# Five of eight images combined, a later lead, and fewer weight steps beside combined images, in a 3x3 convolution with quantised weights and group normalisation

## The chip, the cores and the metric

The kernel runs on one core of one Trainium2 chip. The metric is the device time of one execution in microseconds (us). The engines are named as the profile names them: PE multiplies matrices, DVE is the vector engine, ACT the scalar engine, POOL is GpSimd, and SP issues transfers.

## The reference

The input x holds 160 images of 128 channels and 32x32 points. Every image is group-normalised (32 groups of 4 channels, over the points too), convolved 3x3 with padding 1, and added to x:

```python
beta, alpha = jnp.max(U), jnp.min(U)
s1 = (beta - alpha) / 3.0
v1 = s1 * floor(U / s1)
s2 = s1 / 5.0
v2 = s2 * floor((U - v1) / s2)
w = (v1 + v2).reshape(128 * 5, 128, 3, 3)
xb = x.reshape(160 // 5, 5 * 128, 32, 32)
act = conv(xb, w, padding=1, feature_group_count=5)
x = x + act.reshape(160, 128, 32, 32)      # conv takes gn(x)
```

There are five sets of weights. The kernel orders the images by set, 32 to a set, so the weights of the next set have to be quantised, turned and summed while the current set is convolved.

## The kernel before, in words

One image is one step of the loop in `run`. Each image is split into a high part (fp16) and a low remainder (fp16), so that products of fp16 matrices keep enough precision. A Winograd-like scheme along one axis turns three taps on two neighbouring rows (or columns) into four products: two of sums and differences, called `m1` and `m2`, and two that go straight to the even and odd outputs. There are two kinds of image.

- An **uncombined image (U)**: only the low part goes through the scheme. GpSimd (`beside_pairs`, L714) or ScalarE (`normalise`, L640) makes the normalised image z; ScalarE casts it to the high part (L648); VectorE subtracts (L751) and makes the three combinations of rows (L764, L772, L773). PE needs 30 matmuls.
- A **combined image (C)**: both parts go through the scheme. GpSimd makes the outer columns and one quarter of the combination v (L678, L708), VectorE the rest (`combine`, L690 and L697); ScalarE scales it to the high part (L738) and VectorE makes the low part in one instruction (`low_combined`, L744). PE needs 24 matmuls.

`combined(i)` chooses: odd images from 7 to 29, then three of five up to image 129 (`THIRDS`), then three of four.

In its step for image i, PE runs the sums of image i+1 (`sums_of_pairs`, into m2 and m1) and then the two halves of image i itself (`main`). ScalarE copies m2 out (`leave`, L891), and VectorE forms the start values of the next image's two banks from m1 and m2 (`pairs`, L903 and L905: the pair update). PE cannot start the halves of an image before its pair update, nor its sums before its low part.

The other work runs ahead by fixed distances. `step_of(i, ahead)` gives the images whose stage is due in step i: stage 4 is GpSimd's work and `combine`, stage 3 the high part, stage 2 the low part. Up to image `FURTHER` the stages run 4, 3 and 2 images ahead; at a certain step each handles two images, and from then on they run 5, 4 and 3 ahead. This extra image is called the lead. Statistics are measured by ScalarE `STAT_LEAD + 1` images ahead (L241, L248).

Quantising the next weights is a list of short VectorE instructions, the weight steps (L142 to L146, L162, L549; sums of taps L573 to L575), 42 per set. `Later` hands them out at a pace; `take(n)` issues up to n that are due. Before the change a step offers three places beside a U image (two around its low part, one after `combine`) and two beside a C image. At the 28th image of a set `later.finish()` issues what is left.

GpSimd's instructions of stage 4 and the power that gives 1/sqrt of the variance (L286) wait for a VectorE instruction named `before`: the last but one of those issued for the low part. All engines run in the written order.

Images are grouped for the statistics, from 24 on by eight. When a group's power is done, VectorE scales it (L307). If the group's first image is U, ScalarE normalises that image (`by_scalar_too`), and VectorE makes a shift for it (L310).

Of the kernel before, what the change touches and what calls it, by code (L numbers as in the profile page):

```python
# [385 lines left out]
class Main:  # L386
# [21 lines left out]

    STAT_LEAD = 15
    FURTHER = 11
    LOAD_LEAD = 18
    CHUNKS = 11
    STEADY = 7
# [193 lines left out]
    def stats_of(self, k):  # L609
        if k not in self.stats:  # L610
            self.stats[k] = Statistics(
                self.nc, self.small, self.gavg, self.mhalf, len(self.groups[k]),
                self.steps.lift, k,
            )
            self.stats[k].late = self.groups[k].start not in self.HURRIED
            self.stats[k].shifted = not self.combined(self.groups[k].start)
        return self.stats[k]

    def measure(self, i, stages=(0, 1)):
# [31 lines left out]
    def combined(self, i):  # L651

        if i < self.STEADY or i >= self.imgs:
            return False

        if i < self.FIFTHS:
            return i % 2 == 1
        return i % 5 % 2 == 0 if i < self.THIRDS else i % 4 != 2

    def by_scalar_too(self, i):  # L660

        return i < self.FIRST + 4 or i == self.groups[self.group_of[i]].start

    def column_of(self, i):

# [307 lines left out]
    def step_of(self, i, ahead):  # L973


        change = self.FURTHER + 4 - ahead
        return [k for k in range(i + ahead + (i > change), i + ahead + 1 + (i >= change)) if k < self.imgs]

    def consumed(self, c):

        return max(i + 2 if self.by_hand(i) else i - 2 - (i > self.FURTHER + 6) for i in range(c * NB, c * NB + NB))

    def run(self):
# [130 lines left out]
        later, turned = Later(), []  # L1114
        for i in range(self.imgs):
            n, b = self.place(i)


            def on_the_way(col):
                if col == self.COLS[1]:  # L1120
                    for st in ready:
                        st.means(self.pg)
                    for *column, parts in self.columns:
                        self.turn_column(*column, parts)
                        turned.append(column)
                    self.columns.clear()
                if col == self.COLS[2]:
                    for st in middle:
                        st.variances()

            if i < self.FIRST:
                if i == self.FIRST - 1:
                    self.sums_of_pairs(self.FIRST)

                j = (i - 1) % self.FIRST
                self.direct_hi(j, self.COLS[2])
                self.direct_lo(j, self.COLS[2])
                if i == 0:
                    self.stats[2].variances()
                    self.stats[2].deviation()  # L1140
                    self.stats[2].power()
                    self.stats[2].scales()
                    run(self.sums_across(0, nc.gpsimd))
                for col in self.COLS:
                    on_the_way(col)
            else:
                j = i - 1
                self.conv(i, on_the_way)
            ahead = i + min(10 + i // 3, self.STAT_LEAD + 1)
            to_measure = range(measured, min(self.imgs, ahead))  # L1150
            measured += len(to_measure)
            if i == 2:
                self.load_set(1)
            if b == self.per_set - 8 and n + 2 < N_SETS:
                self.load_set(n + 2)
            if n + 1 < N_SETS:
                if b == (4 if n == 0 else 1):
                    later = Later(
                        (s for col in self.COLS for s in self.make_column(n + 1, col, "later")),
                        36 / (self.per_set - 6 - b),  # L1160
                    )
            later.next_image()
            by_scalar = [k for k in to_measure if not self.by_vector(k)]
            by_vector = [k for k in to_measure if self.by_vector(k)]

            if i < self.FIRST:

                if i == 0:
                    measure(0, 8, 9, 10)
                if i == 1:  # L1170
                    self.normalise(4)
                    self.high_part(4)
                if i == 2:
                    self.leave(3)
                    self.normalise(5)
                    measure(1, 9)
                    self.high_part(5)
                    self.pairs(3)
                    self.low_part(4)
                    run(self.combinations(4))  # L1180
                    measure(0, 11)
                self.residual(j)
            else:

                last = None
                for k in self.step_of(i, 2):
                    if self.combined(k):
                        last = last_of(self.low_combined(k), last)
                    else:
                        self.low_part(k)  # L1190
                        later.take(1)
                        last = last_of(self.combinations(k), last)
                last = later.take(1, last)
                if last:
                    before = self.last_but_one(last)
                    for st in scaled:
                        self.after(st.power(), before)
                    for k in self.step_of(i, 4):
                        self.beside_pairs(k, before)
                if i > self.FIRST and self.by_hand(j):  # L1200
                    self.residual(j)
                for k in by_scalar:
                    self.measure(k, (0,))
                if i > self.FIRST and not self.by_hand(j):
                    self.residual(j)
                    self.accumulate(j)
                if i + 1 < self.imgs:
                    self.leave(i + 1)
                for st in ready:
                    if not st.late:  # L1210
                        st.deviations()
                for k in self.step_of(i, 3):
                    if self.combined(k):
                        self.high_combined(k)
                        continue
                    if self.by_scalar_too(k):
                        self.normalise(k)
                    self.high_part(k)
                for k in by_scalar:
                    self.measure(k, (1,))  # L1220
            for st in middle:
                st.deviation()
                if not st.late:
                    st.power()
                    st.scales()
            if i < self.FIRST:
                for st in ready:
                    st.deviations()
            for n_of, col in turned:
                self.keep_taps(n_of, col)  # L1230
                if col == self.COLS[-1]:
                    later = Later(self.sums_of_set(n_of), 3.0)
            turned = []

            if i >= self.FIRST:

                if i + 1 < self.imgs:
                    self.pairs(i + 1)
                for st in scaled:
                    st.scales_by_vector()  # L1240
                for k in self.step_of(i, 4):
                    if self.combined(k):
                        self.combine(k)
                    later.take(1)
                later.take_scalar()
                if b in (self.per_set - 4, self.per_set - 2):
                    later.finish()
                for st in ready:
                    if st.late:
                        st.deviations_by_vector()  # L1250
            scaled, middle, ready = [st for st in middle if st.late], ready, []
            if i >= self.FIRST:
                measure(0, *by_vector)
            for k in to_measure:
                group = self.group_of[k]
                if k + 1 == self.groups[group].stop:
                    ready.append(self.stats[group])
            while loaded * NB < self.imgs and (
                loaded * NB < i + self.LOAD_LEAD if loaded < self.CHUNKS
                else i >= self.consumed(loaded - self.CHUNKS)  # L1260
            ):
                self.load(loaded)
                due.append((i + 4, loaded))
                loaded += 1
            if due and due[0][0] <= i:
                self.store_input(due.pop(0)[1])
# [49 lines left out]
```

## Time and profile before

| | |
|---|---|
| median of three runs | 966.23 us (966.21 to 966.47) |
| the profiled execution | 964.56 us |
| its span | 962.5 us |
| PE busy | 927.8 us, 96% |
| DVE busy | 902.6 us, 94% |
| ACT busy | 862.7 us, 90% |
| POOL busy | 460.1 us, 48% |

The span lies between the first and the last instruction; the rest of the execution is around it. Matmuls are pipelined, so the busy share of PE counts overlapping ones as one stretch; the spacing of their starts tells their pace.

### The profile page before, as it was taken

What the parts mean: (1) busy time and instruction counts of PE and PEld (TensorE: products, weight loads), DVE (VectorE), ACT (ScalarE), POOL (GpSimd) and SP (SyncE); (2) the same over time, 40 slices, a digit from 0 to 9 for tenths busy, and PEclk for the clock granted to TensorE, in tenths of its full rate; (3) what the DMA queues carried; (4) which work ended last, traced back from release to release, by engine and by line L of the source; (5) the groups of instructions that cost most, each with busy time, mean ns of one, the idle gap of its engine ahead of it and who ended that gap; (6) DMA issues with size and microseconds to landing.
All of it is one profiled execution on the core that took longest, in us unless ns stands there. A gap on an engine that the chain in (4) does not pass through costs nothing.

```text
span 962.5 us, 13034 instructions
## 1 busy us (share of the span) xinstructions
PE 927.8 (96%) x4432; PEld 433.8 (45%) x4432; DVE 902.6 (94%) x1269; ACT 862.7 (90%) x1167; POOL 460.1 (48%) x477
## 2 busy tenths in 40 slices
PE   2899989999999999999999999999999999999997
PEld 1344434444444444444444444444444444444443
DVE  7989999999899999989999999899999998999993
ACT  5879989999899999999999999999999999997660
POOL 4344434456445445554545445545444366565640
PEclk9999999999999999999999999999999999999999
DMA  9079999999999999999999999999999999856563
GB/s 349 36 267 345 334 348 320 325 321 325 328 321 323 317 295 308 272 306 254 295 251 289 284 293 297 282 277 286 267 273 267 282 279 269 172 91 107 91 107 112
DMA packets 67450, 254.22 MB, mean 264 GB/s; under 512 B 5296, under 2 KB 5296, under 8 KB 67376
## 3 DMA queue, kind: packets, MB, share of 16 engines
q1 hardware_dynamic: 45344, 173.09, 48.0%
q0 software_dynamic: 22032, 80.23, 44.4%
q8 instruction: 36, 0.59, 0.2%
q14 instruction: 38, 0.31, 0.1%
HBM read 89.19 MB, written 164.10 MB: 263 GB/s over the span
## 4 chain that ended last, share of the span: by engine, by line


## 5 line engine op out<-in xcount | busy, mean ns | idle before, releaser
L788 PE MATMUL eo<-hi,wt 128*128 128x496 f16 (+3 forms) x1170 | 310.8, 376 | 2.4 <-DVE eo L905 1.7
L843 PEld LDWEIGHTS <-wt 128*128 128x128 f16 x1884 | 183.9, 99 | 211.5 <-DVE eo L905 2.7
L744 DVE SCALAR_TENSOR_TENSOR vl<-v,rstd,vh 128x2048 f16<-128x2048 f32 x94 | 221.8, 2360 | 0.2 <-ACT vh L738 0.2
L843 PE MATMUL eo<-vh,wt 128*128 128x512 f16 x561 | 210.1, 375 | 1.2 <-DVE eo L905 1.2
L843 PE MATMUL eo<-vl,wt 128*128 128x512 f16 x561 | 210.1, 374 | 0.0
L738 ACT ACTIVATE vh<-v,rstd 128x2048 f16<-128x2048 f32 x94 | 188.2, 2002 | 4.8 <-DVE v L697 4.3
L929 ACT COPY sum<-eo 128x1024 f32<-128x1024 f32 x153 | 161.0, 1052 | 32.3 <-PE eo L843 31.7
L788 PEld LDWEIGHTS <-wt 128*128 128x128 f16 x1242 | 121.2, 99 | 142.8 <-DVE eo L905 4.9
L678 POOL TENSOR_SCALAR v<-xt,ngm 128x64 f32<-128x64 f32 x94 | 79.1, 842 | 202.0 <-DVE vl L744 86.9
L248 ACT ACTIVATE junk<-xt,mv 128x1024 uint8<-128x1024 f32 x152 | 174.4, 1148 | 0.3
L241 ACT ACTIVATE junk<-xt 128x1024 uint8<-128x1024 f32 x152 | 160.5, 1056 | 13.3 <-DMA xt<-in_x_dram 10.0
L714 POOL TENSOR_SCALAR z<-xt,ngm,rstd 128x1024 f32<-128x1024 f32 x49 | 93.3, 1904 | 165.1 <-DVE rows L773 55.0
L843 PEld LDWEIGHTS <-across 128*128 128x128 f16 x1128 | 110.8, 98 | 131.9 <-issue 4.9
L843 PE MATMUL eo<-rows,wt 128*128 128x512 f16 x378 | 143.5, 380 | 0.0
L953 POOL DMA_DIRECT2D out_dram<-sum x153 | 133.7, 874 | 14.4 <-ACT sum L929 6.6
L690 DVE TENSOR_TENSOR v<-xt 128x960 f32<-128x960 f32 x94 | 114.0, 1212 | 0.0
L843 PE MATMUL m<-vl,across 128*128 128x496 f16 (+1 forms) x282 | 106.4, 377 | 2.1 <-DVE vl L744 2.1
L891 ACT ACTIVATE m<-m 128x512 f32<-128x512 f32 x157 | 93.7, 597 | 14.1 <-PE m L843 13.7
L843 PE MATMUL m<-vh,across 128*128 128x496 f16 (+1 forms) x282 | 106.2, 376 | 0.2 <-ACT m L891 0.2
L708 POOL TENSOR_TENSOR v<-xt 128x512 f32<-128x512 f32 x94 | 97.2, 1034 | 0.0
L751 DVE TENSOR_TENSOR lo<-z,hi 128x1024 f16<-128x1024 f32 x66 | 80.6, 1221 | 0.0
L286 POOL TENSOR_TENSOR rstd<-ve,mhalf 128x8 f32<-128x8 f32 (+2 forms) x24 | 42.3, 1761 | 65.1 <-DVE rows L773 21.1
(150 smaller groups left out, 1166.3 us busy)
## 6 DMA issues: line engine op xcount, KB each, us to landing
xt<-in_x_dram SPq DMA_DIRECT2D x78, 1024.0 KB, 9.6
out_dram<-sum POOLq DMA_DIRECT2D x153, 512.0 KB, 8.7
out_dram<-xt SPq DMA_DIRECT2D x76, 1024.0 KB, 14.2
out_dram<-xt SPq DMA_DIRECT2D x7, 512.0 KB, 3.3
u<-in_L_conv_U_dram SPq DMA_DIRECT2D x4, 576.0 KB, 13.6
xt<-in_x_dram SPq DMA_DIRECT2D x4, 512.0 KB, 10.1
range<-in_L_conv_U_dram SPq DMA_DIRECT2D x3, 576.0 KB, 8.3
u<-in_L_conv_U_dram SPq DMA_DIRECT2D x2, 288.0 KB, 3.1
```

What stands on the lines that cost most here:

```text
L241: self.nc.scalar.activation(junk, image, ACTF.Copy, scale=-1.0 / image.shape[1], accum_out=self.mv[:, j, 0:1],)
L248: self.nc.scalar.activation(junk, image, ACTF.Square, bias=self.mv[:, j, 0:1], accum_out=self.mv[:, j, 1:2],)
L690: nc.vector.tensor_tensor(self.view(v, 1, (511, 2), (half, H), (1, half - 1)), self.view(x, 1, (1, 2), (W, H), (2, half - 1)), self.view(x ...
L708: ins = nc.gpsimd.tensor_sub(self.v[i][:, 1536:], odd, even)
L714: ins = nc.gpsimd.tensor_scalar(z, self.image(i), st.ngm[:, j], st.rstd[:, j], ALU.add, ALU.mult)
L738: self.nc.scalar.mul(vh, self.v[i], st.rstd[:, j])
L744: yield self.nc.vector.scalar_tensor_tensor(vl, self.v[i], st.rstd[:, j], self.hi[i], ALU.mult, ALU.subtract)
L788: nc.tensor.matmul(self.bank(target, a)[:, first:end, c0:c1], self.wts[n, col][:, k, :], tile[:, s0 : s0 + 2 * (end - first) - 1 : 2, c0 + ...
L843: self.nc.tensor.matmul(out, weights, moving, start=start and j == 0, stop=False, skip_group_check=True)
L891: self.nc.scalar.mul(m2, self.m2_ps, 0.5)
L929: nc.scalar.copy(self.as_banks(i, self.sum[i]), self.flat(i, eo))
L953: added = self.nc.gpsimd.dma_start(self.ov[n, :, b], self.sum.pop(i), accum_op=ALU.add)
```

## The change

Six edits. The lead is built at image 33 and no longer at 11 (`FURTHER`). Of images 30 to 129, those with `i * 5 % 8 < 5` are combined (residues 0, 2, 4, 5, 7 of eight) in place of three of five. After the low part no weight step is offered when image i+3 is combined, and in that case `before` is the last instruction itself, not the last but one. Statistics run one image further ahead from image 30 on. ScalarE normalises only first images of groups that start before image 40, and GpSimd the others; the shift goes with it.

```diff
-    STAT_LEAD = 15
-    FURTHER = 11
+    STAT_LEAD = 16
+    BY_SCALAR = 40
+    FURTHER = 33
...
-            self.stats[k].shifted = not self.combined(self.groups[k].start)
+            start = self.groups[k].start
+            self.stats[k].shifted = start < self.BY_SCALAR and not self.combined(start)
...
-        return i % 5 % 2 == 0 if i < self.THIRDS else i % 4 != 2
+        return i * 5 % 8 < 5 if i < self.THIRDS else i % 4 != 2
 
     def by_scalar_too(self, i):
 
-        return i < self.FIRST + 4 or i == self.groups[self.group_of[i]].start
+        start = self.groups[self.group_of[i]].start
+        return i < self.FIRST + 4 or i == start and start < self.BY_SCALAR
...
-            ahead = i + min(10 + i // 3, self.STAT_LEAD + 1)
+            ahead = i + min(10 + i // 3, 16 if i < 30 else self.STAT_LEAD + 1)
...
-                last = later.take(1, last)
+                last = later.take(0 if self.combined(i + 3) else 1, last)
                 if last:
-                    before = self.last_but_one(last)
+                    before = last.ins if self.combined(i + 3) else self.last_but_one(last)
```

## The prediction

> **What bounds the kernel now.** I read the busy table first, then the stretches of time, PE's spacing in the timeline, and last VectorE and GpSimd around one end of a group.
>
> ```profile
> PE 927.8 (96%) x4432; PEld 433.8 (45%) x4432; DVE 902.6 (94%) x1269; ACT 862.7 (90%) x1167; POOL 460.1 (48%) x477
> ```
>
> PE is the bound on average, VectorE (DVE) two points behind. The busy time by stretch shows where PE loses time:
>
> ```profile
> 120.00:160.00 40.00, 36.05 (x161) 15.79 (x160) 39.55 (x64) 36.27 (x50) 13.38 (x15) 0.96 1.04 337
> 480.00:540.00 60.00, 59.53 (x290) 27.96 (x289) 58.91 (x81) 57.89 (x81) 28.30 (x29) 1.00 0.99 277
> ```
>
> From 120 to 160 us DVE is busy 39.55 of 40 us while PE is not; there the lead is built, and DVE is the bound. Later PE is full. How much room DVE has then is in its waits from 225 to 797 us (images 30 to 130):
>
> ```profile
> DVE eo L903 <- PE m1b L843: 9.1, 8, 2.5
> DVE eo L903 <- ACT m L891: 4.5, 6, 1.3
> DVE eo L903 <- PE m1a L843: 4.3, 6, 1.4
> DVE rstd L307 <- POOL rstd L286: 2.0, 9, 0.2
> ```
>
> 20 us of 572: DVE has 3.5% in hand. PE's own cost per image, from its timeline:
>
> ```profile
> 500.68 0.80 PE L788 MATMUL eo<-hi,wt 128*128 128x512 f16 x3
> ...
> 505.79 0.38 PE L843 MATMUL m<-vh,across 128*128 128x512 f16 x1
> ...
> 508.32 0.38 PE L843 MATMUL eo<-vh,wt 128*128 128x512 f16 x1
> ...
> 510.86 0.81 PE L843 MATMUL m<-rows,wt 128*128 128x512 f16 x3
> ...
> 512.16 0.38 PE L843 MATMUL eo<-vh,wt 128*128 128x512 f16 x1
> ```
>
> From start to start: halves of a U image 5.11 us, sums of a C image 2.53, halves of a C image 2.54, sums of a U image 1.30. So C costs 5.07 and U 6.41; one image made C saves PE 1.34. Counting pair updates, PE starts image 77 at 495.60 and image 117 at 722.51: 226.91 us for 24 C and 16 U (224.24), 0.66 of stall and so 2.0 of weight turns and statistics, 0.05 per image.
>
> The end of a group, VectorE and then GpSimd:
>
> ```profile
> 437.14 2.34 DVE L744 SCALAR_TENSOR_TENSOR vl<-v,rstd,vh 128x2048 f16<-128x2048 f32 x1
> 439.40 0.61 DVE L144 SCALAR_TENSOR_TENSOR tt<-tt,s1r,nnn 128x384 f32<-128x384 f32 x1
> ...
> 441.57 0.37 DVE L307 TENSOR_SCALAR rstd<-rstd,lift 128x8 f32<-128x8 f32 x1 [0.22 <-POOL rstd L286]
> 441.95 1.99 DVE L690 TENSOR_TENSOR v<-xt 128x960 f32<-128x960 f32 x1
> ```
>
> ```profile
> 439.64 1.90 POOL L286 TENSOR_TENSOR rstd<-ve,mhalf 128x8 f32<-128x8 f32 x1 [2.38 <-DVE vl L744]
> 441.54 0.37 POOL L678 TENSOR_SCALAR v<-xt,ngm 128x64 f32<-128x64 f32 x1
> 441.88 1.03 POOL L708 TENSOR_TENSOR v<-xt 128x512 f32<-128x512 f32 x1
> ```
>
> L690 takes 1.99 us here and 1.15 elsewhere: it ends 1.03 after L708 does. The power ends 1.53 after the weight step L144 (440.01); over all groups of eight that distance from the instruction behind the gate is 1.51 to 1.56.
>
> **What the skill says.** The Trainium skill, "SBUF — State Buffer", section "Who interferes with whom": a VectorE instruction with two SBUF inputs and a GpSimd instruction that reads SBUF exclude each other for the whole instruction, whoever starts first. The trace agrees: 1.99 against 1.15 us. "TensorE: Matmul & The Clock Gate", section "What's actually happening": PE runs at half rate after an idle window of about 3.4 us. Here it did so after 2.3 us of near idleness: from 129.88 to 132.8 matmuls start 0.41 us apart instead of 0.21. No page bears on the order of the weight steps.
>
> **The parts.** DVE's costs from start to start of the next instruction: pair update 1.34, `combine` 1.73, low part of C 2.26, low part of U 2.45, weight step 0.51 on average (sums of taps 0.33), group statistics 0.55, scaling 0.20.
>
> (a) *Lead not built at 11.* At image 14 DVE makes two low parts between two pair updates, 10.97 us. PE goes from image 13 (124.25) to 14 (134.63), 10.38 us for 2.54 + 2.53 of work: 5.3 lost, the half rate within. Another 1.1 goes at 157.39. In the changed order this step has one low part (C), no `combine` and one weight step, and three weight steps fewer stand in the rows before (1.5 us). The low part of image 15 then ends near 126.6 and PE is free for it at 126.8. The next four rows need 6.5 + 5.8 + 7.6 + 4.1 = 24.0 of DVE against 23.2 of PE, so about 1.4 of stall stays. Gain 6.4 − 1.4 = **5.0** (4 to 6). Without the lead PE's sums depend on a low part of the same row; that wait is in the 1.4.
>
> (b) *Weights finished at image 28 of set 0.* The changed order has six sums of taps in one row, 1.96 us, ahead of the low part of image 31. From the pair update of 29: 1.73 + 1.96 + 2.26 = 5.95, against PE's margin (1.5 to 3.3) plus 2.54. Stall 0.1 to 1.9; I take **1.8**, as the early rows leave little margin.
>
> (c) *Lead built at 33.* The row of image 36 gets scaling, `combine`, two low parts (C, U), three weight steps and the pair update: 0.2 + 1.73 + 2.26 + 2.45 + 1.7 + 1.34 = 9.7, plus 1.5 of wait at the group's end (d), 11.2. PE needs 5.11 + 2.53 + 0.05 = 7.7 meanwhile. The margin before it is 2.3 (seen at image 35) to 3.5 (the most possible: 2.54 + 2.53 less 1.34 and 0.25 of latency). Row 37: 5.9 against 3.9. Stall 2.0 to 3.2, against 0.44 in the kernel before at image 37: 1.6 to 2.8, I take **2.6**.
>
> (d) *Images 40 to 129.* Two more images of 100 are C: PE −2.68, DVE + 2 x (1.73 + 2.26 − 2.45) = +3.1. ScalarE loses five normalisations of 1.27 (images 48, 56, 88, 96, 128), which only widens its waits. These five do not go to GpSimd: with the new pattern every group that starts from 32 to 128 starts with C. So the GpSimd edit moves nothing, cost 0; dropping the shift saves 5 x 0.09. But now all group ends have `combine` right behind the scaling, where five of twelve had not. And no weight step stands behind the low part of C any more, while `before` is that low part itself. So the power starts 0.16 after it and takes 1.53; the scaling waits 0.4; L678 and L708 end at 3.1, and L690 at 4.1 where it could have ended at 2.5: **1.5** per group. The bounds: 0, where DVE waits for PE anyway (as at 395 and 622 us), and 1.9, if the power's 1.90 holds. At other C rows L708 reaches 0.11 into L690: the one such case in the trace (785.84 to 788.35) had L690 at 1.26.
>
> Per 32 images DVE then needs 32 x 1.34 + 20 x 1.73 + 20 x 2.26 + 12 x 2.45 + 36 x 0.51 + 6 x 0.33 + 4 x 0.75 = 175.6, plus 4 x 1.5 and 8 x 0.11 = 182.5. PE needs 20 x 5.07 + 12 x 6.41 + 32 x 0.05 = 179.9. DVE becomes the bound by 2.6. The same sum for 40 images before gives 221, and the trace 226.91 − 6.3 of waits = 220.6. At 182.5/32 = 5.70 the 90 images take 513.2 against 510.6 now (285.26 to 795.87): +2.6. Rows without weight steps, where DVE still waits for PE, add 1.2: **3.8**.
>
> (e) *Statistics one image further, loads one step later from 18 to 39.* One extra measurement, 2.3 us of ScalarE at step 30, beside the stall of (b); transfers land in a median of 9.6 us and are read six steps, some 34 us, later. 0; if the cover of (b) is gone, up to 1.
>
> Sum: −5.0 + 1.8 + 2.6 + 3.8 = +3.2. On the profiled execution, 964.56 + 3.2 = 967.8; the median lies 1.67 above that execution, so **969.4 us**. A difference under 0.2%, 1.9 us, is what measurement can't tell from none.
>
> **The rivals.** *Group ends are hidden* and PE stays the bound: (d) is −2.7, the sum −3.3, 962.9 us. It decides once a group end costs DVE less than 0.87 (175.6 + 0.9 + 4 x 0.87 = 180). For it: two of the seven such ends now are covered by a wait. Against: DVE's hand is 3.5% and the change spends it. *PE falls to half rate* in the stalls of (b) and (c): at 127 us this added some 1.8, so 971 to 973. Against: a stall of 1.1 at 157 did not. *Both single rows are absorbed*: (b) 0, (c) 0.5, sum −0.7, 965.5; needs margins at their most. *The change doesn't do what it says* holds for the GpSimd edit alone, at no cost.
>
> **The numbers.** Chances: forecast 0.50 (its own range 967.5 to 972), half rate 0.12, absorbed 0.18, hidden 0.20. Of the forecast 0.04 falls within 0.2%. So faster 0.20, same 0.22, slower 0.58. The range runs from the middle of the hidden case, 962.8, to 973.0.
>
> **What would show it.** (a) No PE stall near 127 us, a granted clock of 1.00 from 120 to 160. (b), (c) PE waits of 1 to 2 us on L744 at image 31 and on the pair update at images 36 and 37. (d) L690 near 2 us at every group end, L307 waiting 0.4, PE waits on L905 of about 1 us per group. Wrong if L690 stays at 1.15 and DVE still waits 20 us for PE in images 40 to 130.

## The result, and the profile after

The changed kernel takes 972.75 us (median of six runs, 971.85 to 973.98) against 966.35 for the kernel before, timed with it: ratio 1.0066, 95% interval 1.0053 to 1.0080. It is 6.4 us slower; the forecast was 3.2 slower, 969.4. One of the six runs of the kernel before took 1655.48 us, for which the record has no cause; without it their median is 966.23. The profiled execution took 971.85 us, its span is 969.7 against 962.5.

In the changed kernel lines from `by_scalar_too` on stand 3 higher: the pair update is L906 and L908, `combine` L693 and L700, the low part of a C image L747, GpSimd's shares L681 and L711; lines of the weight steps from L549 on stand 1 higher. The busy table:

```profile
PE 928.2 (96%) x4420; PEld 432.3 (45%) x4420; DVE 915.2 (94%) x1262; ACT 857.3 (88%) x1162; POOL 397.8 (41%) x484
```

PE is as busy as before although it has 12 fewer instructions. VectorE gained 12.6 us of busy time with 7 fewer instructions: two more combined images, and single instructions that take longer, above all the first of `combine`, which from image 40 to 130 takes about 1.99 us ten times where it did so four times before (1.15 is its usual time). The same two stretches as before (span, then busy time of PE, PEld, DVE, ACT, POOL, then clock, DMA share, GB/s):

```profile
120.00:160.00 40.00, 38.09 (x181) 17.41 (x180) 39.49 (x65) 38.11 (x53) 11.91 (x14) 1.00 1.04 330
480.00:540.00 60.00, 59.51 (x286) 27.67 (x285) 58.49 (x77) 56.98 (x81) 27.22 (x31) 1.00 1.00 278
```

From 120 to 160 us PE is now busy for 38.09 of 40 us instead of 36.05, at a clock of 1.00 instead of 0.96. The gain of (a) lies there. What VectorE waits for from 225 to 797 us:

```profile
DVE rstd L307 <- POOL rstd L286: 5.1, 10, 0.5
DVE eo L906 <- PE m1a L846: 3.6, 5, 1.1
DVE eo L906 <- ACT m L894: 2.5, 3, 1.3
```

Together with 0.6 for ScalarE at one image, the 20 us of before have become 12, of which 5.1 are a wait for GpSimd at ten ends of a group. And PE, which there waited for the pair update three times (1.2 us), now waits like this (228 to 805 us):

```profile
PE eo L846 <- DVE eo L908: 5.9, 7, 2.0
PE m L846 <- DVE across L575: 1.7, 3, 0.6
PE small L559 <- DVE m L550: 1.5, 3, 0.5
```

The second and third rows are new: PE waits for sums of taps at images 64, 96 and 128, and at images 43, 75 and 107 for the last weight step before a turn of weights (PE transposes a column of the quantised weights, L559; there are three turns to a set). One end of a group, VectorE and then GpSimd:

```profile
252.97 0.70 DVE L908 SCALAR_TENSOR_TENSOR eo<-m1b,m 128x512 f32<-128x512 f32 x1
254.18 0.37 DVE L307 TENSOR_SCALAR rstd<-rstd,lift 128x8 f32<-128x8 f32 x1 [0.51 <-POOL rstd L286]
254.55 1.99 DVE L693 TENSOR_TENSOR v<-xt 128x960 f32<-128x960 f32 x1
...
257.77 2.36 DVE L747 SCALAR_TENSOR_TENSOR vl<-v,rstd,vh 128x2048 f16<-128x2048 f32 x1
```

```profile
252.48 1.66 POOL L286 TENSOR_TENSOR rstd<-ve,mhalf 128x8 f32<-128x8 f32 x1 [1.46 <-DVE vl L747]
254.15 0.37 POOL L681 TENSOR_SCALAR v<-xt,ngm 128x64 f32<-128x64 f32 x1
254.49 1.03 POOL L711 TENSOR_TENSOR v<-xt 128x512 f32<-128x512 f32 x1
```

As the forecast had it: the power runs 1.66, VectorE waits 0.51 for it, then L693 takes 1.99 while L711 runs. That VectorE and GpSimd shut each other out here is called the lock below. 0.51 + 1.99 − 1.15 = 1.35 per end; 1.5 was forecast. PE at image 36, where the lead is now built:

```profile
262.67 0.37 PE L846 MATMUL m1b<-vl,across 128*128 128x496 f16 x1
264.99 0.55 PE L846 MATMUL eo<-vh,wt 128*128 128x512 f16 x1 [1.95 <-DVE eo L908]
265.34 0.63 PE L846 MATMUL eo<-vl,wt 128*128 128x512 f16 x1
265.76 0.62 PE L846 MATMUL eo<-vh,wt 128*128 128x496 f16 x1
...
268.60 0.37 PE L846 MATMUL eo<-vl,wt 128*128 128x496 f16 x1
```

From 262.67 to the next start are 2.32 us where 0.21 is the pace: a stall of 2.11. Then the starts lie about 0.42 apart up to 268.27: PE runs at half rate. The nine spacings from 264.99 to 268.60 take 3.61, which costs another 3.61 − 9 x 0.2125 = 1.7.

The time by stages, from the starts of an image's halves in PE's timeline (11, 18, 30, 40 and 130), for this and all the kernels below; the last column is the span:

```
                       to 11  11-18  18-30  30-40  40-130  130-end   span
before                112.47  46.27  69.75  56.77  510.61   166.63  962.5
after                 112.09  42.93  71.92  60.41  515.89   166.46  969.7
undo_lead             113.28  47.45  69.75  56.33  515.86   166.53  969.2
undo_gate             113.53  42.94  71.73  60.10  512.10   167.20  967.6
undo_steps            112.94  43.24  70.38  61.26  511.00   166.48  965.3
undo_pattern          112.94  43.24  70.86  66.67  522.25   166.44  982.4
undo_stat             113.10  43.22  71.93  62.88  514.16   166.71  972.0
lead_30               112.89  43.23  71.92  58.09  516.01   166.56  968.7
only_pattern          113.76  47.76  69.75  56.32  510.63   167.08  965.3
reorder               113.11  42.51  70.86  60.11  509.09   167.02  962.7
combine_only          113.47  43.35  72.06  60.56  517.18   166.48  973.1
before_reorder        114.45  45.58  69.75  56.33  509.31   166.68  962.1
reorder_lead30        112.88  42.47  70.87  57.79  509.22   166.47  959.7
reorder_steps_lead30  112.25  41.85  70.37  57.41  506.61   166.61  955.1
```

Of the 7.2 us between the spans of before and after: −0.4 ahead of image 11, −3.3 from 11 to 18, +2.2 to 30, +3.6 to 40, +5.3 to 130, −0.2 behind. Each row is one execution. The first column differs by 2.4 us among kernels, and the second by 1.5 between before (46.27) and only_pattern (47.76), whose order of work is the same up to there; differences of that size in these two columns show nothing. From 18 to 130 the columns repeat to a few tenths where the order of work is the same.

### The profile page after: what moved, and what is told of

It reads as the page before. It is cut to its first block, busy times and chain, and to the rows that moved or that the text cites. A ratio compares the mean times of both kernels' runs of the same rounds, so it can differ in the third digit from the quotient of the medians.

```text
span 969.7 us, 12991 instructions
## 1 busy us (share of the span) xinstructions
PE 928.2 (96%) x4420; PEld 432.3 (45%) x4420; DVE 915.2 (94%) x1262; ACT 857.3 (88%) x1162; POOL 397.8 (41%) x484
## 4 chain that ended last, share of the span: by engine, by line
## 5 line engine op out<-in xcount | busy, mean ns | idle before, releaser
L791 PE MATMUL eo<-hi,wt 128*128 128x512 f16 (+1 forms) x1134 | 301.9, 376 | 0.9 <-ACT wt L570 0.9
L747 DVE SCALAR_TENSOR_TENSOR vl<-v,rstd,vh 128x2048 f16<-128x2048 f32 x96 | 225.8, 2352 | 0.3 <-ACT vh L741 0.3
L846 PE MATMUL eo<-vh,wt 128*128 128x512 f16 x573 | 215.7, 376 | 6.0 <-DVE eo L908 5.9
L846 PE MATMUL eo<-vl,wt 128*128 128x512 f16 x573 | 215.6, 376 | 0.0
L741 ACT ACTIVATE vh<-v,rstd 128x2048 f16<-128x2048 f32 x96 | 192.4, 2004 | 25.7 <-DVE v L700 25.4
L241 ACT ACTIVATE junk<-xt 128x1024 uint8<-128x1024 f32 x152 | 160.7, 1057 | 12.6 <-DMA xt<-in_x_dram 9.3
L681 POOL TENSOR_SCALAR v<-xt,ngm 128x64 f32<-128x64 f32 x96 | 45.7, 476 | 266.9 <-DVE vl L747 111.9
L717 POOL TENSOR_SCALAR z<-xt,ngm,rstd 128x1024 f32<-128x1024 f32 x52 | 64.7, 1245 | 195.7 <-DVE vl L747 119.9
L846 PE MATMUL eo<-rows,wt 128*128 128x512 f16 x366 | 138.9, 380 | 0.0
L693 DVE TENSOR_TENSOR v<-xt 128x960 f32<-128x960 f32 x96 | 124.8, 1300 | 0.0
L711 POOL TENSOR_TENSOR v<-xt 128x512 f32<-128x512 f32 x96 | 98.9, 1031 | 0.0
L700 DVE SCALAR_TENSOR_TENSOR v<-xt,twice 128x512 f32<-128x512 f32 x96 | 71.3, 743 | 0.0
```

The costliest lines, as they stand in the source:

```text
L241: self.nc.scalar.activation(junk, image, ACTF.Copy, scale=-1.0 / image.shape[1], accum_out=self.mv[:, j, 0:1],)
L693: nc.vector.tensor_tensor(self.view(v, 1, (511, 2), (half, H), (1, half - 1)), self.view(x, 1, (1, 2), (W, H), (2, half - 1)), self.view(x ...
L711: ins = nc.gpsimd.tensor_sub(self.v[i][:, 1536:], odd, even)
L741: self.nc.scalar.mul(vh, self.v[i], st.rstd[:, j])
L747: yield self.nc.vector.scalar_tensor_tensor(vl, self.v[i], st.rstd[:, j], self.hi[i], ALU.mult, ALU.subtract)
L791: nc.tensor.matmul(self.bank(target, a)[:, first:end, c0:c1], self.wts[n, col][:, k, :], tile[:, s0 : s0 + 2 * (end - first) - 1 : 2, c0 + ...
```

## The experiments

The theory was the prediction's own: gains and costs in four places, (a) to (d), of which (d) comes from VectorE running out of room at the ends of groups. Each kernel below is the changed one with the edit shown, unless it says otherwise. They were timed in three series, the first four below up to undo_pattern, then undo_stat, lead_30, only_pattern and reorder, then the rest; the kernel before took 966.66, 966.9 and 966.54 us in them. Each ratio is the recorded one against those runs; it can differ by up to 0.0008 from the quotient of the two medians. What is called faster or slower than the kernel before rests on intervals that leave out 1; kernels of different series are compared by their medians.

### The lead at 11 again (undo_lead)

```diff
-    FURTHER = 33
+    FURTHER = 11
```

> The changed kernel with the lead built at image 11 again, all else as changed. Theory (costs add up by place: late lead loses 4.1 us of PE at images 36 and 37, and saves about 3.0 between images 13 and 18): both go, so the time moves by 3.0 - 3.7 = about -0.7 us, to 972; PE stalls return near 127 us and those near 262 us go. Rival (the late lead is what makes the kernel slower): 966 to 968 us.

970.95 us, ratio 1.0040 (1.0026 to 1.0055): 1.8 us below the changed kernel, a little below the theory's 972 and well above the rival's 966 to 968. The table says why so little: from 11 to 18 the early lead costs 4.5 us more (47.45 against 42.93), from 30 to 40 it saves 4.1, and from 18 to 30 it saves 2.2 that the prediction had not put to it: the waits at 163.05 us (1.02) and at image 31 (1.06) are gone. In the stretch from 120 to 160 us the clock falls again:

```profile
120.00:160.00 40.00, 36.23 (x162) 15.98 (x161) 39.59 (x65) 34.49 (x45) 11.72 (x14) 0.91 1.04 339
```

### The gate as before (undo_gate), and gate and steps as before (undo_steps)

```diff
-                    before = last.ins if self.combined(i + 3) else self.last_but_one(last)
+                    before = self.last_but_one(last)
```

> The changed kernel with GpSimd's stage-4 work waiting for the last but one instruction of the low part again, all else as changed. Theory (group ends cost what the power's late start adds): power and L681 start beside the low part and get the port when it ends, the group end costs VectorE 0.5 us less and every other combined row 0.1 to 0.2 less; the six stalls at images 53, 61, 85, 93, 117, 125 shrink; -3 to -4 us, 969. Rival (the gate only moves a wait of GpSimd that is covered): 0, 972.7.

968.3 us, ratio 1.0013 (1.0006 to 1.0020), 4.45 below the changed kernel, a little more than expected. GpSimd's work is released one instruction earlier, so the power is issued beside the low part (251.24 to 253.58), ends 1.5 us after it, and is nearly done when VectorE wants it; GpSimd, then VectorE:

```profile
251.47 3.63 POOL L286 TENSOR_TENSOR rstd<-ve,mhalf 128x8 f32<-128x8 f32 x1
```

```profile
255.14 0.37 DVE L307 TENSOR_SCALAR rstd<-rstd,lift 128x8 f32<-128x8 f32 x1 [0.22 <-POOL rstd L286]
255.52 1.98 DVE L693 TENSOR_TENSOR v<-xt 128x960 f32<-128x960 f32 x1
```

The wait fell from 0.51 to 0.22, L693 stayed at 1.98. Small as that is, images 40 to 130 take 3.8 us less: PE's stalls at images 53, 85 and 117 are gone, those at 61, 93 and 125 fell from 1.3 to 0.8, and the waits for a turn of weights from 0.66 to 0.37.

In undo_steps the offer of a weight step behind every low part comes back too:

```diff
-                last = later.take(0 if self.combined(i + 3) else 1, last)
+                last = later.take(1, last)
```

> The changed kernel with both edits at the weight steps undone (a place for a step behind every low part, and the last but one as the gate). Theory: weight steps end earlier, so the waits of PE on the turned weights (0.66 x 3) and on the sums of taps (0.73 x 3) go, 4.2 us, and the gate's share as in the run that undoes it alone; rows of combined images get heavier; -4 to -7 us, 966 to 969. Rival (fewer steps beside combined images smooth VectorE and are worth something): slower than the run that undoes the gate alone.

967.31 us, ratio 1.0008 (0.9999 to 1.0017), another 1.0 below, within the theory's range. The waits for sums of taps and for the turn of weights are gone; the stalls at images 53, 85 and 117 are back at 1.2 each. So leaving the steps out costs about 1 us and saves nothing, though the two intervals overlap.

### Three of five again (undo_pattern), and only the pattern (only_pattern)

```diff
-        return i * 5 % 8 < 5 if i < self.THIRDS else i % 4 != 2
+        return i % 5 % 2 == 0 if i < self.THIRDS else i % 4 != 2
```

> The changed kernel with three of five images combined again from 30 to 129. Theory (VectorE is over PE by 2.6 us per 32 images, of which the pattern is 0.8): PE gains 2.7 us of work, VectorE loses 3.1, ScalarE and GpSimd change little; stalls at group ends get smaller; -1 to +1 us, 972 to 974. Rival (the two extra combined images make the slowdown): 966 to 968.

983.6 us, ratio 1.0168 (1.0149 to 1.0187). Neither expectation holds. At the first turn of weights VectorE is still making sums of taps when PE needs them; VectorE's timeline, then PE's:

```profile
233.41 0.35 DVE L574 TENSOR_TENSOR across<-wt 128x384 f16<-128x384 f16 x1
233.79 0.36 DVE L575 TENSOR_TENSOR across<-across,wt 128x384 f16<-128x384 f16 x1
```

```profile
234.21 0.61 PE L846 MATMUL m<-vh,across 128*128 128x512 f16 x1 [4.47 <-ACT junk L241]
```

PE resumes at 234.21, just after L575 has made the second sum `across` (233.79 to 234.15); the ScalarE instruction named in the bracket is only the last event of several. PE's stops for turns and sums of taps are 4.63 at image 32, 1.47 and 3.30 about image 64, 1.34 and 1.60 about 96, 0.86 and 0.44 about 128, 13.6 us in all. With the new places the third turn of each set comes late whatever the pattern: PE makes it during images 29, 61, 93 and 125 here, during 28, 61, 93 and 125 in the changed kernel, and during 26, 59, 91 and 123 in the kernel before. That the old pattern then costs so much more in nearly the same rows fits its places standing in other spots of the row, but no run shows this by itself. The edits of the pattern and of the places are tied to each other, and undoing one of them doesn't measure it. So the pattern was also tried alone, in the kernel before:

```diff
-        return i % 5 % 2 == 0 if i < self.THIRDS else i % 4 != 2
+        return i * 5 % 8 < 5 if i < self.THIRDS else i % 4 != 2
```

> The kernel before with one edit alone: from image 30 to 129 five of eight images are combined, not three of five; lead, weight steps, statistics and GpSimd as before. Theory: PE saves 2.68 but VectorE pays 3.1 for two more combined images and takes over the bound, so this part alone gives no gain: 966 to 968.5. Rival: VectorE's 20 us of waits in this stretch absorb it and PE's saving comes out: 963.5 to 964.5. A second rival: as with the pattern undone, the weight steps then fit badly into the rows and PE waits for sums of taps: over 971.

966.63 us, ratio 1.0000 (0.9991 to 1.0009). From image 40 to 130 it takes 510.63 us against 510.61: PE's saving of 2.68 is used up, most of it in stalls of 1.2 at images 53, 85 and 117. The time is the theory's, and neither rival's, but the theory's cost for VectorE is too small: in this stretch VectorE is busy for 501.30 us against 491.50, 9.8 more and not 3.1. Most of the rest is in the first instruction of `combine` (L690); its busy time in the kernel before, then here:

```profile
285.26:795.87 510.61, 65.64 (x54) 1.00 1.02 286
287.59:798.22 510.63, 73.75 (x56) 1.00 1.01 284
```

Two more of them account for 2.3 us of these 8.1. The others come from the lock: with the new pattern every group starts with a C image, and L690 takes 1.99 us eleven times where it did so four times. The pattern brings the costly ends of groups with it.

### Statistics (undo_stat) and another place for the lead (lead_30)

```diff
-    STAT_LEAD = 16
+    STAT_LEAD = 15
```

> The changed kernel with STAT_LEAD = 15 from image 30 on as well. Theory (e): the statistics' lead is worth nothing, 971.5 to 973.5, with the stall at image 31 (1.06) unchanged. Rival: the extra measurement at image 30 delays ScalarE there, and the stall at image 31 falls by up to 1: 970.5 to 971.5.

972.54 us, ratio 1.0060 (1.0040 to 1.0080); the stall at image 31 is 1.06 still. In time this is nothing, as expected, but only because two shifts nearly cancel: 2.5 more from 30 to 40, where one stall of 3.48 at image 37 brings half rate with it, and 1.7 less from 40 to 130. The second one has a cause for which the prediction's (e) has no term. With statistics one image less ahead, every end of a group from image 30 on falls one row later, in the rows of images 35, 43, 51 and so on, and not of 34, 42, 50. There i+3 is uncombined (46 and not 45), so the edit at the gate doesn't apply, and VectorE waits 0.22 for the power and not 0.51 (228 to 805 us; the changed kernel has 5.1 us there):

```profile
DVE rstd L307 <- POOL rstd L286: 2.6, 12, 0.2
```

So the gate lengthens the ends of groups only because the statistics edit puts them into rows where i+3 is combined.

```diff
-    FURTHER = 33
+    FURTHER = 30
```

> The changed kernel with FURTHER = 30, so that the lead is built three images earlier. Theory (c): the stall of 2.11 at image 36 and the half rate behind it (together about 4.1 us) come from two low parts standing in one row beside a group's end; in another row the stall is below 1.5 and the half rate goes: 968.5 to 970.5. Rival: the lead costs VectorE the same wherever it is built, and the stall only moves: 972 to 973.

970.59 us, ratio 1.0046 (1.0034 to 1.0058), a tenth above the theory's range and below the rival's. From 30 to 40 it takes 58.09 us instead of 60.41; the largest stall there is 1.17, and no half rate follows. Some 2.3 of the 3.6 us that the late lead costs depend on the row in which it is built. That this row is dear because of the end of a group fits; the two rows differ in their weight steps too, which was not separated.

### The end of a group without the lock (reorder, combine_only, before_reorder)

Not in the change: GpSimd's shares go ahead of the power, and VectorE's `combine` ahead of the scaling.

```diff
-                    for st in scaled:
-                        self.after(st.power(), before)
                     for k in self.step_of(i, 4):
                         self.beside_pairs(k, before)
+                    for st in scaled:
+                        self.after(st.power(), before)
...
-                for st in scaled:
-                    st.scales_by_vector()
                 for k in self.step_of(i, 4):
                     if self.combined(k):
                         self.combine(k)
                     later.take(1)
+                for st in scaled:
+                    st.scales_by_vector()
```

> Not part of the change: of the changed kernel, but in each row GpSimd's shares of the new v and z are issued ahead of the power, and VectorE's combine stands ahead of the scaling, so that the power is behind VectorE's next work. Theory (d): the lock beside the scaling makes each of some ten ends of a group 0.8 us longer (1.99 against 1.15 us), and 0.4 to 0.5 us of wait goes with it; taken away, the PE waits at images 53, 61, 85, 93, 117 and 125 (3 x 0.38 + 3 x 1.28 = 5.0 us) go: 967 to 968.5. Rival: the late weight steps are what delays PE; the waits of 0.66 at each turn of weights and of 0.73 for sums of taps stay and VectorE's freed time ends in other waits: 971 to 972.5.

963.81 us, ratio 0.9968 (0.9961 to 0.9976): about 9 us below the changed kernel, 3.2 below the theory's range, and faster than the kernel before. The same end of a group, VectorE and then GpSimd:

```profile
253.46 0.70 DVE L908 SCALAR_TENSOR_TENSOR eo<-m1b,m 128x512 f32<-128x512 f32 x1
254.06 1.25 DVE L693 TENSOR_TENSOR v<-xt 128x960 f32<-128x960 f32 x1
...
256.88 0.23 DVE L307 TENSOR_SCALAR rstd<-rstd,lift 128x8 f32<-128x8 f32 x1 [0.25 <-POOL rstd L286]
257.02 2.34 DVE L747 SCALAR_TENSOR_TENSOR vl<-v,rstd,vh 128x2048 f16<-128x2048 f32 x1
```

```profile
252.92 0.38 POOL L681 TENSOR_SCALAR v<-xt,ngm 128x64 f32<-128x64 f32 x1 [1.42 <-DVE vl L747]
253.26 1.03 POOL L711 TENSOR_TENSOR v<-xt 128x512 f32<-128x512 f32 x1
254.27 2.58 POOL L286 TENSOR_TENSOR rstd<-ve,mhalf 128x8 f32<-128x8 f32 x1
```

L711 now runs beside the pair update and is over when L693 starts; L693 takes 1.25. The power instead meets `combine` and takes 2.58, but only the scaling waits for it, 0.25. From the end of the pair update to the next low part VectorE needs 257.02 − 254.16 = 2.86 us, where the changed kernel needed 257.77 − 253.67 = 4.10 for the same instructions: 1.24 less per end. The stalls on the pair update behind image 37 are gone (5.0 us), and, which was not expected, so are the waits of 0.66 for each turn of weights (2.0) and the stall at image 31 (1.06): they depended on the order at the ends of groups as well. At images 36 and 37, where the lead is built, 1.40 and 1.95 stay, without half rate. The waits for sums of taps stay too, 0.54, 0.55 and 1.38, as the rival said; its figure for the time falls.

One of the two moves alone, with the power still first:

```diff
-                for st in scaled:
-                    st.scales_by_vector()
                 for k in self.step_of(i, 4):
                     if self.combined(k):
                         self.combine(k)
                     later.take(1)
+                for st in scaled:
+                    st.scales_by_vector()
```

> Not part of the change: of the changed kernel, VectorE's combine stands ahead of the scaling; the power stays ahead of GpSimd's shares. This takes the wait for the power (0.4 to 0.5 us at each group's end) away and leaves the lock. Theory: the lock is the larger part, combine then only starts earlier and still ends with GpSimd's share, so little is won: 970 to 972.5, against 963.8 with both moves. Rival: the wait for the power is what costs; without it the time falls as with both moves: 963.5 to 967.

974.59 us, ratio 1.0082 (1.0064 to 1.0100), slower than expected and slower than the changed kernel. VectorE's waits from 228 to 805 us begin with

```profile
DVE v L693 <- POOL v L681: 9.1, 11, 0.9
```

The wait for the power is gone from L307 and stands at L693, 9.1 us in place of 5.1: `combine` needs GpSimd's share, which is still behind the power, and L693 still takes 1.99. Moving `combine` alone doesn't get rid of the lock. The other move alone, GpSimd's shares ahead of the power with the scaling still first, was not tried.

Both moves, made in the kernel before (the diff of reorder):

> The kernel before with the same two moves (shares ahead of the power, combine ahead of the scaling). Theory: ends of a group cost only where VectorE has no room; in the kernel before it had 20 us of waits from image 30 to 130 and PE lost under 2 us there, so the moves are worth at most that: 964.5 to 966.5. Rival: the moves shorten the kernel by as much as they did in the changed one (8.9 us): 957 to 960.

963.1 us, ratio 0.9968 (0.9958 to 0.9977). This is 3.4 us faster, more than the theory allowed and far less than the rival. From 228 to 805 us PE has no wait left, and 40 to 130 take 509.31 us, 1.3 less than before. From image 11 on the two profiles differ by 2.4 us, 0.7 of it from 11 to 18, where executions differ by more than that anyway; the rest of the 3.4 is not seen in them.

### Together (reorder_lead30, reorder_steps_lead30)

To the two moves of reorder comes the lead at 30:

```diff
-    FURTHER = 33
+    FURTHER = 30
```

> The changed kernel with both moves and FURTHER = 30. Theory: what the lead costs and what the ends of groups cost add up; of the 3.36 us that PE still waits at images 36 and 37 about half goes: 961 to 963. Rival: the stall only moves: 963.5 to 964.5.

961.46 us, ratio 0.9947 (0.9928 to 0.9965): the two costs add up, 2.3 us less from 30 to 40 than in reorder and 0.1 more from 40 to 130.

And to that, gate and steps as they were in the kernel before:

```diff
-                last = later.take(0 if self.combined(i + 3) else 1, last)
+                last = later.take(1, last)
...
-                    before = last.ins if self.combined(i + 3) else self.last_but_one(last)
+                    before = self.last_but_one(last)
```

> The changed kernel with both moves, FURTHER = 30, and the weight steps as in the kernel before (one behind each low part, and the gate one instruction earlier). Theory: weight steps come early enough, the waits for sums of taps at images 64, 96 and 128 (0.55 to 1.38 us) go, and rows lose nothing since VectorE has room again: 960 to 962. Rival: a weight step beside a combined image costs VectorE what it saves later: as without this edit, 961.5 to 963.5.

958.19 us, ratio 0.9918 (0.9899 to 0.9936), 8.35 us faster than the kernel before and the fastest of all; it beats the rival's figure and the lower end of the theory's. Here the pattern, the lead (at 30) and the two moves are kept, and gate and weight steps are as they were. From 228 to 805 us PE waits once, 0.5 us, and VectorE waits for PE:

```profile
DVE eo L906 <- PE m1a L846: 12.6, 12, 1.9
DVE eo L906 <- ACT m L894: 2.6, 6, 1.2
```

From image 64 to 96 it takes 179.91 us; the prediction's sum for PE alone was 179.9. And from 40 to 130 it takes 506.61 against 509.31 in before_reorder, which has the old pattern and, like this kernel, no wait of PE in that stretch: 2.70 less, where the prediction's saving of PE by two more combined images was 2.68. Now that VectorE has room, the pattern gives what it can.

## Why the prediction was right and where it was off

The sign, the mechanism of (d) and the range hold, the range only just: 972.75 lies 0.25 us inside its end. The forecast time is 3.35 us too low, and the change is twice the forecast one; (a), (c) and (d) all came out dearer than forecast. (The profiled executions differ by more than the medians, 7.2 against 6.4, and the stages below are theirs.)

**(a) The lead not built at 11** was forecast at −5.0 and gave −3.3 from image 11 to 18. The half rate near 127 us is gone, as said. What was mis-sized is the rest: 1.4 us of stall was to stay in the next rows (the figures given, 24.0 against 23.2, leave 0.8, and where the other 0.6 comes from isn't said), and 0.57 + 1.06 + 0.79 = 2.4 stayed at 127, 139 and 148 us. A part of the miss is the execution: against the profile of only_pattern, whose order is that of the kernel before up to there, the gain is 4.8. Behind image 18 a wait of 1.02 at 163 us is new, for which the step has no term. GpSimd's group statistics (L267) there meet a low part of VectorE and take 2.20 us; with the lead at 11 they took 0.50. An early lead, undo_lead shows, pays back 2.2 of its cost from image 18 to 30, this wait and the stall of (b). The prediction had counted it as a pure loss.

**(b) The stall at image 31** was forecast at 1.8 within 0.1 to 1.9, and measured 1.06, with the six sums of taps ahead of the low part as forecast.

**(c) The lead at 33** was forecast at 2.0 to 3.2 of stall. The stall at image 36 is 2.11, at 37 it is 0.27. The rival of half rate happened here and added 1.7, so that the step is +3.6 against 2.6. The prediction gave this rival a chance of 0.12 and 971 to 973 us, which is where the time lies; but it added nothing at (b), and by itself it explains 1.7 of the 3.35.

**(d) Images 40 to 129** were forecast at +3.8 and gave +5.3. The sum by 32 images was about right: 182.5 forecast for VectorE, 183.03 measured from image 64 to 96, of which VectorE waits 1.3 for PE and ScalarE; it was 179.31 before. (As written the terms give 175.4 and not 175.6, which changes little.) The ends of groups cost 1.35 in place of 1.5. Wrong was where PE would feel it: about 1 us per group on the pair update was forecast, some 4 per 32 images. In fact 0.38 + 1.28 per 32 images falls there, and 0.66 + 0.73 falls on weight steps that come late, at the turn and at the sums of taps. The sum of rows had no place for a due time. In reorder three of the four are gone, so they depend on the order at the ends of groups; the last, the sums of taps, goes only when gate and weight steps are as before (undo_steps, reorder_steps_lead30).

**Which edit it was.** only_pattern, undo_steps and undo_gate part (d) further than the prediction did, in this order: with the pattern alone 0.0, with gate and steps of before but the other edits +0.4, with the steps left out +1.5, with the gate moved as well +5.3. The prediction laid the loss on the pattern's ends of groups together with the gate, and both are in the runs. The pattern's own saving of 2.68 goes into its ends of groups, which is why it gives 0.0. The gate, put last, adds 3.8; it does so together with the statistics edit, which moves the ends of groups into rows where the gate differs (undoing that edit alone gives 1.7 back). The gate was not tried alone in the kernel before, so these shares hold for this order of edits only.

**(e) Statistics** at 0 came out in time by luck: 1.7 us of the +5.3 of (d) go with the statistics edit undone, and a longer stall at image 37 takes them back. The prediction had a term for one extra measurement and none for the row in which a group ends. "The GpSimd edit moves nothing" follows from the code, since every group from image 40 on starts with a C image; no run undoes this edit.

**The rivals.** Hidden group ends (962.9) fall for this change: an end cost 1.35, and the rival needed less than 0.87. What it says of the condition fits reorder, which takes 1.24 of each end away and needs 963.81; that this lies near 962.9 is in part chance, since images 40 to 130 give −1.5 there and not −2.7. Absorbed single rows (965.5) fall with 1.06 at image 31 and 2.11 at 36. The Trainium skill, "SBUF — State Buffer", section "Who interferes with whom", carried the main term, and the runs agree: L693 takes 1.25 when GpSimd's share is over before it and 1.99 when L711 runs beside it.

## What to carry to other kernels

Before moving work from one engine to another that is nearly as busy, look at what else moves with it: here five of eight combined images gave 0.0 us alone, because they made VectorE's instructions longer at the ends of groups, and 2.7 once these were in order. Before taking work out, look at an instruction that is longer in some places than in others, and at what the other engine reads at that time; the order of two instructions on each of two engines won back more than all six edits had cost. An edit that only shifts when something is done, as the statistics edit here, can decide in which row two other things meet. And when one edit is undone, ask what else was sized for it: the old pattern with the new places for weight steps was the slowest kernel of all.

## What was not expected of the hardware

Half rate of PE after a stall has no sharp bound in these traces. Single stalls up to 1.96 us were never followed by it, one of 3.48 and ones of 3.30 and 4.63 were; in between it went both ways: after 2.11, 2.24, two of 2.43 and two of 2.59 it came, after 2.27, another 2.43 and one of 2.60 it did not. Between 1.4 and 2.9 us were lost each time. The Trainium skill, "TensorE: Matmul & The Clock Gate", section "What's actually happening", has an idle window of about 3.4 us; here a stall of 2.11 was enough.

And executions of equal beginnings differ: near 90 us eleven of the fourteen profiles show PE waiting 1.3 to 1.9 us for ScalarE, among them kernels whose order there is the same as in those that don't. The profiles of before and after are both among the three without this wait. Why it comes was not tested. It is a quarter of what this change costs, and a reason to compare stages rather than spans.
